# Routing spread over the projection in single steps, with VectorE and TensorE pinned to program order, in a decoder layer with a mixture of experts

## The chip, the core and the metric

The kernel runs on one core of one Trainium2 chip. A core has five engines with a queue each: TensorE (PE: matrix products and transposes), VectorE (DVE), ScalarE (ACT), GpSimd (POOL) and SyncE (SP, which only issues transfers here); POOL issues the gathers, which take their row numbers from a table. Each engine works off its queue in order and waits for the others by semaphores. The metric is the device time of one execution in microseconds (us), lower is better.

## The reference

A decoder layer on 16 sequences of 100 tokens of width 512 (1600 tokens): causal self-attention, cross-attention to 361 context rows for each sequence, and a feed-forward part with 8 experts, two for each token. A layer norm follows each part. The change touches the output product of the cross-attention, its layer norm, and the feed-forward part:

```python
# cross-attention, end
out = out.transpose(0, 2, 1, 3).reshape(b, s, NH * HD)   # 16 heads of 128
return out @ Wo                                          # 2048 x 512
...
# feed-forward, x is the normed sum
logits = jnp.einsum('bsd,de->bse', x, router_w) + router_b
topk_vals, topk_idx = jax.lax.top_k(logits, 2)
topk_w = jax.nn.softmax(topk_vals, axis=-1)
full_w = jnp.sum(one_hot(topk_idx, 8) * topk_w[..., None], axis=-2)
h = jnp.einsum('td,edf->etf', xf, expert_w) + expert_b[:, None, :]
combined = jnp.einsum('etf,te->tf', silu(h), full_w)
out = combined @ proj_w + proj_b
y = x + out
return norm_w * (y / sqrt(mean(y * y) + EPS))
```

With two choices, the softmax of the two greatest logits is a pair of gates g1 and g2 = 1 - g1.

## The kernel before

**Precision.** Most products are made of three: each operand is split into a high part (a cast, `split`, L135) and the rest (a subtraction, L142), and `mm3` (L145) sums high by high, high by low and low by high. The cast runs on ACT as a rule, the subtraction on DVE or POOL. So each operand of PE costs one operation on ACT and one on DVE or POOL.

**The output product.** The 1600 tokens are 13 tiles of 128 (the last has 64). A *part* (t, g) is tile t by head group g of four heads: `d_part` (L878) makes 4 x 3 products of 512 columns into the tile's sum `acc`. The list `parts` goes tile by tile for tiles 0 to 9 and then, for the last `TAIL` = 3 tiles, group by group: (10,0), (11,0), (12,0), (10,1) and so on; parts 40 to 51. `d_load(i+1)` (L869) is written ahead of `d_part(i)`: it fetches the heads (`of`) and splits them into `ot`, a pair with two buffers, with the subtraction on DVE for odd parts and on POOL for even ones. Behind the last group of a tile follows `d_norm` (L898): the residual is fetched and added, statistics on DVE, logarithm and exponential on ACT, the scaling on DVE, a store to `x2d`.

**Logits.** `d_turn(t)` (L980) transposes a normed tile on PE, copies it on ACT, adds the projection's bias on POOL and stores that to `xbd`. `d_logits` (L996) gives four small products, which are set among the products of a part, and one addition on DVE (`lg`).

**Routing** is exact and all on the chip. `choose(a, b)` (L1110) finds the two greatest logits for tiles a to b-1, and each token's rank in its expert: a chain of small DVE operations, then products with triangular matrices on PE into `gb`, then a second chain. `settle(a, b)` (L1204) assigns tiles of 128 places (slots) to experts, some 40 DVE operations on tables of 72 to 648 columns. `slots` (L1306) makes the row numbers `idx` and the offsets of each slot's expert (`wat`, `bat`) from 36 or more products of one or few columns. The first 9 tiles (`CUT`) are settled early and give the first 11 slots (`EARLY`) of 32; the other 21 slots need all 13 tiles.

**Experts.** The weights of expert e are split into slot e of an arena that holds `Wo`, too, so that four experts wait for the last part that reads their place (`load_expert`, L1389). For slot i, `e_gather` (L1348) fetches 128 rows by index on POOL's queue, `e_turn` (L1352) transposes them on PE and splits them on ACT and DVE, `e_product` (L1360) makes 12 products with weights at an offset read from `wat`, `e_bias` (L1373) fetches a bias on SP, `e_out` (L1378) adds it on DVE, applies silu on ACT and stores. After 32 slots each token's two rows are gathered, weighed by g1 and g2, projected and normed; that stage is not touched.

**Order.** The program is traced in the order of the code, and a scheduler then orders the instructions of each engine by priority (by place in the code, unless `tc.high_priority(offset=...)` lifts them) and by the times at which a model of the chip has them ready. `in_turn` (L122) adds an order between two instructions without a semaphore. In the code the routing is written as whole functions: `choose` behind tiles 3, 6 and 9, `settle` and `slots` behind part 39, `choose(CUT, CUT + 1)` behind part 42; the second round, for the last three tiles, behind expert product 2.

Of the kernel before, what the change touches and what calls it, by code (L numbers as in the profile page):

```python
# [63 lines left out]
def tile_decoder_layer(  # L64
# [69 lines left out]

    def split(dst, src, high=None, low=None):  # L135

        high, low = high or nc.scalar, low or nc.vector
        if high is nc.scalar:
            ins = nc.scalar.copy(dst.h, src)  # L139
        else:  # L140
            ins = high.tensor_copy(dst.h, src)  # L141
        low.tensor_tensor(dst.l, src, dst.h.bitcast(FP), ALU.subtract)  # L142
        return ins
# [836 lines left out]
    def d_turn(t):  # L980
        t0, n = TT[t]
        x2 = X2.pop(t)
        pt = bank("t", [128, KC, 128], f"ptx2_{t}")
        for k in range(KC):
            nc.tensor.transpose(
                pt[:, k, :n], x2[:n, k * 128 : (k + 1) * 128], ident[:n, :n]
            )
        if t < NT - 1:
            XT2[t] = w1.tile([128, KC, 128], FP, name=f"x2f_{t}", tag="x2f")
        else:  # L990
            XT2[t] = raw[:, 0].rearrange("p (k n) -> p k n", n=128)
        nc.scalar.copy(XT2[t][:, :, :n], pt[:, :, :n])
        nc.gpsimd.tensor_tensor(x2[:n], x2[:n], pb[:n], ALU.add)
        nc.sync.dma_start(xbd[t][:n], x2[:n])
# [114 lines left out]

    def choose(a, b):  # L1110
# [5 lines left out]
        for j in range(2):  # L1116

            nc.vector.tensor_reduce(top[:, j, a:b], vals, AX.X, ALU.max)
            hit = table("hit", sh)
            nc.vector.tensor_tensor(  # L1120
                hit, vals, top[:, j, a:b].unsqueeze(2).to_broadcast(sh), ALU.is_equal
            )
            nc.vector.tensor_tensor(hit, hit, num_b, ALU.mult)
            nc.vector.tensor_reduce(place[:, j, a:b], hit, AX.X, ALU.min)
            nc.vector.tensor_tensor(
                one[:, j, a:b, :],
                num_b,
                place[:, j, a:b].unsqueeze(2).to_broadcast(sh),
                ALU.is_equal,
            )  # L1130
            if j == 0:
                rest = table("rest", sh)
                nc.vector.scalar_tensor_tensor(
                    rest, one[:, 0, a:b, :], -BIG, vals, ALU.mult, ALU.add
                )
                vals = rest
        if b == NT:

            nc.vector.memset(one[64:, :, NT - 1, :], 0.0)
        nc.vector.tensor_tensor(  # L1140
            chosen[:, a:b, :], one[:, 0, a:b, :], one[:, 1, a:b, :], ALU.add
        )
        for t in range(a, b):
            nc.vector.tensor_tensor(
                cum[:, t + 1, :], cum[:, t, :], chosen[:, t, :], ALU.add
            )
        o1, o2 = 2 * NE, (2 + m) * NE
# [21 lines left out]
        )  # L1169
        sh2 = [128, 2, m, NE]  # L1170
# [6 lines left out]
        )  # L1177
        rj = gw.tile([128, 2, m], FP, name=f"rj_{a}", tag=f"rj_{m}")
        nc.vector.tensor_reduce(rj, mine, AX.X, ALU.add)
        ri = gw.tile([128, 2, m], I32, name=f"ri_{a}", tag=f"ri_{m}")  # L1180
        nc.vector.tensor_copy(ri, rj)
        nc.vector.tensor_scalar(ri, ri, 127, None, ALU.bitwise_and)
        nc.vector.tensor_copy(lo[:, :, a:b], ri)

        nc.vector.tensor_scalar(rj, place[:, :, a:b], float(NE), None, ALU.add)
        nc.vector.scalar_tensor_tensor(
            opens[:, :, a:b], lo[:, :, a:b], 0.0, rj, ALU.is_equal, ALU.mult
        )
        if b == NT:
            nc.vector.memset(opens[64:, :, NT - 1 :], 0.0)  # L1190
            nc.vector.memset(token[64:, NT - 1 :], 0.0)

        for j in range(2):
            for t in range(a, b):
# [7 lines left out]
                )  # L1202

    def settle(a, b):  # L1204
# [5 lines left out]
        if a == 0:  # L1210
            by_128(full, count[:, m, :], "full")

        up = table("up", [128, m + 1, NE])
        nc.vector.tensor_scalar(up, count, 127.0, None, ALU.add)
        had = table("had", [128, m + 1, NE])
        by_128(had, up, f"had_{a}")

        opn = table("opn", sh)
        nc.vector.tensor_tensor(opn, had[:, 1:, :], had[:, :m, :], ALU.subtract)
        had = had[:, :m, :]  # L1220
        sh4 = [128, m, NE, NE]

        def before_it(these, here, less, name):
# [7 lines left out]
            )  # L1231
            new = table(name, sh)
            nc.vector.tensor_reduce(new, part, AX.X, ALU.add)
            nc.vector.tensor_reduce(here[:, a:b], these, AX.X, ALU.add)
            tri = parts_of([128, 1, m, b])[:, 0]
# [5 lines left out]
            )  # L1241
            till = table("till", [128, m])
            nc.vector.tensor_reduce(till, tri, AX.X, ALU.add)
            nc.vector.scalar_tensor_tensor(
# [6 lines left out]
            )  # L1251
            return new


        new = before_it(opn, opened, 0 if a else -EARLY, "new")
        if a == 0:
# [3 lines left out]
            )  # L1260
            nc.vector.tensor_tensor(fills, fills, opn, ALU.mult)
            first = before_it(fills, filled, 0, "first")
# [3 lines left out]
            )  # L1266

            nc.vector.scalar_tensor_tensor(
                fills, first, float(EARLY), fills, ALU.is_lt, ALU.mult
            )  # L1270
            nc.vector.tensor_tensor(first, first, new, ALU.add)
            nc.vector.tensor_tensor(first, first, fills, ALU.mult)
            nc.vector.tensor_tensor(new, first, new, ALU.subtract)

        nc.vector.tensor_tensor(places[:, a:b, :], opn, new, ALU.mult)
        sh5 = [128, m, NE, b]
# [6 lines left out]
        )  # L1283
        old = table("old", sh)
        nc.vector.tensor_reduce(old, prior, AX.X, ALU.max)
        nc.vector.tensor_tensor(new, new, old, ALU.subtract)

# [3 lines left out]
        )  # L1291
        nc.vector.tensor_tensor(new, new, past, ALU.mult)
        nc.vector.tensor_tensor(new, new, old, ALU.add)
        sh3 = [128, m, NSL]
        for j in range(2):
            mine = table("chose", sh)
            nc.vector.tensor_tensor(mine, one[:, j, a:b, :], new, ALU.mult)
            nc.vector.tensor_reduce(tile_of[:, j, a:b], mine, AX.X, ALU.add)
            nc.vector.tensor_tensor(
# [4 lines left out]
            )  # L1304

    def slots(a, b, upto):  # L1306
# [4 lines left out]
        inv, who = gb[:, o1:o2], gb[0:1, o2:]  # L1311
        for dst, of in ((inv, named), (who, opens.unsqueeze(3))):
# [9 lines left out]
        nc.vector.tensor_copy(idx, inv)  # L1322
        wat = k1.tile([1, m], I32, name=f"wat_{a}")
        nc.vector.tensor_scalar(wat, who, float(KC * D), None, ALU.mult)
        bat = k1.tile([1, m], I32, name=f"bat_{a}")
        nc.vector.tensor_scalar(bat, who, float(D), None, ALU.mult)
        for i in range(a, b):
# [61 lines left out]
    def load_expert(e, last=False):  # L1389
        for k in range(KC):  # L1390
# [10 lines left out]
            )  # L1401

    for i in range(HEAD * NKV, len(parts)):
# [4 lines left out]
        if t < NT - TAIL:  # L1408
            if g == 1:
# [10 lines left out]
        elif (t, g) == (NT - 1, NKV - 1):  # L1420
            d_turn(NT - TAIL)
        d_part(i, among)
        if g == NKV - 1:
            with tc.high_priority(offset=URGENT if t >= NT - TAIL else 0):
                d_norm(t)
# [4 lines left out]
        if t % 3 == 0 and t <= CUT and g == 3:  # L1430
            choose(t - 3, t)
        if (t, g) == (NT - 1, 0):
            choose(CUT, CUT + 1)
        if (t, g) == (CUT, 3):
            settle(0, CUT)
            slots(0, EARLY, CUT)
        if (t, g) == (NT - 1, 1):
# [4 lines left out]
    load_expert(wo_slot[3], True)  # L1442
    e_turn(0)
    e_turn(1)
    e_product(0, d_logits(NT - TAIL))
    with tc.high_priority(offset=URGENT):
        d_turn(NT - 2)
        d_turn(NT - 1)
    e_turn(2)

    def at_once(t):
        with tc.high_priority(offset=URGENT):
            for f in d_logits(t).values():
                f()

    e_product(1, {1: lambda: at_once(NT - 1)})
    e_turn(3)
    e_product(2, {0: lambda: at_once(NT - 2)})
    d_l.close()
    e_l = ExitStack()  # L1460
    ebb = pool(e_l, "ebb")
    for i in range(TAIL):
        e_bias(i)
    for i in range(TAIL):
        e_out(i)
    with tc.high_priority(offset=URGENT):
        choose(CUT + 1, NT)
        settle(CUT, NT)
        slots(EARLY, NSL, NT)
    slot_f = gw.tile([128, 2 * NT], FP, name="slot_f")  # L1470
    nc.vector.scalar_tensor_tensor(
        slot_f,
        tile_of.rearrange("p j t -> p (j t)"),
        128.0,
        lo.rearrange("p j t -> p (j t)"),
        ALU.mult,
        ALU.add,
    )
    slot = k1.tile([128, 2, NT], I32, name="slot")
    nc.vector.tensor_copy(slot.rearrange("p j t -> p (j t)"), slot_f)  # L1480
    ex = gw.tile([128, NT], FP, name="ex")
    nc.vector.tensor_tensor(ex, top[:, 1, :], top[:, 0, :], ALU.subtract)
    nc.scalar.activation(ex, ex, AF.Exp)
    g1 = k1.tile([128, NT], FP, name="g1")
    nc.vector.tensor_scalar(g1, ex, 1.0, None, ALU.add)
    nc.vector.reciprocal(g1, g1)
    g2 = k1.tile([128, NT], FP, name="g2")
    nc.vector.tensor_tensor(g2, ex, g1, ALU.mult)
# [284 lines left out]
    for i in range(NSL + 1):  # L1773
        if i + 4 < NSL:
            e_gather(i + 4)
# [3 lines left out]
        if TAIL <= i < NSL:  # L1779
            e_product(i)  # L1780
            e_out(i)
        if i == EARLY + 1:
# [102 lines left out]
```

## Time and profile before

| what | us |
|---|---|
| three runs of the kernel | 1400.23, 1400.51, 1403.87 |
| the profiled execution | 1408.13 |
| its span, first to last instruction | 1406.4 |
| PE busy | 1331.6 |
| DVE busy | 942.8 |
| ACT busy | 756.4 |
| POOL busy | 710.3 |

The profile comes from one execution and has several views. The table of engines gives busy time for each engine; the table by stage gives the same for chosen stretches, with the clock that TensorE was granted (1.00 is full). The list of waits tells which instruction ended an engine's idle time. The timeline gives start, duration, engine, line, operation, output and inputs of each instruction, and in brackets the idle time ahead of it with what ended it; on PE the durations of neighbours overlap, and the pace is read from one start to the next. `acc` is the sum of a tile, `ot_h` and `ot_l` its split heads, `xs` and `xsT` gathered rows as they come and turned, `ph` an expert product, `parts`, `new`, `old` and `hit` tables of the routing.

In the profile the last product of tile 9 starts at 1161.0 us, the last part ends at 1205.2, and the product of slot 11 starts at 1260.9. Routing of the first 9 tiles ran on DVE from 1163 to 1201, that of the last three from 1225 to 1252.

### The profile page before, as it was taken

The numbers are of one execution on the slowest core, as the hardware profiler recorded it, in microseconds if no ns is written. First come the engines' busy times: TensorE is split into PE (matmuls) and PEld (weight loads), VectorE is DVE, ScalarE is ACT, GpSimd is POOL, SyncE is SP. The second block draws the span as 40 slices with busy tenths as digits, with TensorE's granted clock in tenths as the row PEclk, the third lists the DMA queues.
The fourth block names the chain that finished last, engine by engine and source line by source line (L and its number), as shares of the span: only waits on it lengthen the run. The fifth ranks groups of instructions, "written<-read, shape, count | busy, mean of one in ns | idle before, by whom it ended". The sixth has DMA issues, their size and how long they took to land.

```text
span 1406.4 us, 25135 instructions
## 1 busy us (share of the span) xinstructions
PE 1331.6 (95%) x7928; PEld 1105.0 (79%) x7928; DVE 942.8 (67%) x2933; ACT 756.4 (54%) x1897; POOL 710.3 (51%) x840
## 2 busy tenths in 40 slices
PE   8999989999999999999999999999999898899894
PEld 7888868888778888888888888878887676677773
DVE  5776677776467777777777767767654558754576
ACT  4666643444446666666666666656654233333356
POOL 6878753344245555555555555545455444532530
PEclk9999989999999999999999999999999999899997
DMA  5221363544442122322233312322446545667883
GB/s 170 68 74 58 124 194 96 131 92 114 100 94 72 42 70 71 76 78 70 71 76 78 74 46 67 73 68 51 118 101 182 178 167 164 211 214 240 256 252 118
DMA packets 199160, 161.74 MB, mean 115 GB/s; under 512 B 133581, under 2 KB 153265, under 8 KB 199029
## 3 DMA queue, kind: packets, MB, share of 16 engines
q1 hardware_dynamic: 189191, 139.77, 36.2%
q0 software_dynamic: 4576, 14.95, 3.4%
q10 hardware_dynamic: 5262, 5.41, 1.3%
q8 instruction: 65, 1.06, 0.3%
q14 instruction: 66, 0.54, 0.1%
HBM read 107.25 MB, written 50.99 MB: 113 GB/s over the span
## 4 chain that ended last, share of the span: by engine, by line
PE 68%; DVE 14%; DMA 7%; ACT 4%; issue 3%; POOL 1%; SPq 1%; ACTq 1%; DVEq 0%; POOLq 0%
PE pq L147 4%; PE pq L148 4%; PE pq L149 4%; PE pv L147 4%; PE pv L148 4%; PE pv L149 4%; PE ptp L819 3%; PE pk L147 3%; PE pk L149 3%; PE pk L148 3%; PE s L147 3%; PE s L148 3%; PE s L149 3%; PE av L148 2%; PE av L147 2%
## 5 line engine op out<-in xcount | busy, mean ns | idle before, releaser
L811 POOL TENSOR_SCALAR p<-p,sums 100x361 f32<-100x361 f32 x256 | 146.4, 577 | 99.4 <-DVE sums L810 88.2
L798 DVE CUSTOM_DVE_ANT_0 p<-s,nmask 100x361 f32<-100x361 f32 x256 | 133.0, 527 | 63.4 <-PE s L149 54.7
L809 ACT ACTIVATE p<-p,nm 100x361 f32<-100x361 f32 x256 | 153.2, 601 | 39.6 <-DVE nm L798 36.3
L142 DVE TENSOR_TENSOR pT_l<-ptp,pT_h 128x400 fp32r<-128x400 f32 (+1 forms) x192 | 107.5, 568 | 57.2 <-ACT pT_h L139 56.8
L147 PE MATMUL pq<-WH 128*128 128x512 f32 (+2 forms) x272 | 107.2, 394 | 5.3 <-DVE WH L141 5.3
L819 PE MATMUL ptp<-ident,p 100*128 100x100 f32 (+1 forms) x768 | 107.4, 252 | 0.0
L139 ACT CAST pT_h<-ptp 128x400 fp32r<-128x400 f32 (+1 forms) x192 | 91.2, 487 | 30.1 <-PE ptp L819 29.7
L142 POOL TENSOR_TENSOR cT_l<-cf,cT_h 128x512 fp32r<-128x512 f32 (+1 forms) x48 | 54.4, 1133 | 103.4 <-ACT cT_h L139 101.5
L819 PEld LDWEIGHTS ptp<-ident,p 100*128 100x128 f32 (+1 forms) x768 | 95.4, 151 | 13.3 <-POOL p L811 2.3
L148 PE MATMUL pq<-WL,WH 128*128 128x512 f32 (+2 forms) x272 | 104.9, 385 | 0.0
L149 PE MATMUL pq<-WH,WL 128*128 128x512 f32 (+2 forms) x272 | 104.6, 385 | 0.0
L149 PE MATMUL acc<-WH,ot_l 128*128 128x512 f32 (+1 forms) x208 | 85.7, 413 | 7.3 <-DVE ot_l L142 5.8
L147 PE MATMUL acc<-WH,ot_h 128*128 128x512 f32 (+1 forms) x208 | 85.1, 409 | 5.0 <-ACT ot_h L139 5.0
L147 PE MATMUL s<-kT_h,WH 128*100 128x362 f32 x256 | 88.1, 355 | 0.7 <-ACT kT_h L139 0.7
L147 PE MATMUL av<-pT_h,WH 128*128 128x400 f32 (+1 forms) x192 | 76.8, 400 | 9.0 <-ACT pT_h L139 8.6
L666 POOL TENSOR_TENSOR qs<-qs,r_q 128x512 f32<-128x512 f32 (+1 forms) x52 | 54.0, 1068 | 60.9 <-DVE r_q L171 49.4
L149 PE MATMUL s<-kT_h,WL 128*100 128x362 f32 x256 | 84.3, 329 | 0.0
L148 PE MATMUL s<-kT_l,WH 128*100 128x362 f32 x256 | 83.7, 327 | 0.0
L148 PE MATMUL acc<-WL,ot_h 128*128 128x512 f32 (+1 forms) x208 | 83.6, 402 | 0.0
L142 POOL TENSOR_TENSOR WL<-qf,WH 128x400 fp32r<-128x400 f32 x64 | 67.3, 1052 | 30.5 <-ACT WH L139 26.9
L147 PE MATMUL pv<-WH,cT_h 128*128 128x512 f32 (+1 forms) x192 | 79.8, 416 | 0.9 <-DVE WL L142 0.9
L148 PE MATMUL pv<-WL,cT_h 128*128 128x512 f32 (+1 forms) x192 | 77.9, 406 | 0.0
(348 smaller groups left out, 3990.6 us busy)
## 6 DMA issues: line engine op xcount, KB each, us to landing
qf<-qd SPq DMA_DIRECT2D x64, 200.0 KB
of<-od SPq DMA_DIRECT2D x48, 256.0 KB
cf<-in_ctxT SPq DMA_DIRECT2D x16, 722.0 KB
eb<-in_expert_b SPq DMA_DIRECT2D x32, 256.0 KB
ysd<-h SPq DMA_DIRECT2D x32, 256.0 KB
f_e<-in_expert_w SPq DMA_DIRECT2D x30, 256.0 KB
f_wq<-in_Wq SPq DMA_DIRECT2D x16, 256.0 KB
f_wo<-in_Wo SPq DMA_DIRECT2D x16, 256.0 KB
```

The costliest lines, as they stand in the source:

```text
L139: ins = nc.scalar.copy(dst.h, src)
L142: low.tensor_tensor(dst.l, src, dst.h.bitcast(FP), ALU.subtract)
L147: nc.tensor.matmul(out, a.h, b.h, start=start, stop=False)
L148: nc.tensor.matmul(out, a.h, b.l, start=False, stop=False)
L149: nc.tensor.matmul(out, a.l, b.h, start=False, stop=stop)
L666: nc.gpsimd.tensor_tensor(qr[:, hs, :], qr[:, hs, :], rs[:n, hs].unsqueeze(2).to_broadcast([n, GR, HD2]), ALU.mult,)
L798: nc.vector.tensor_tensor_reduce(out=p, in0=sc[:, :SE], in1=nmask, scale=1.0, scalar=BIG, op0=ALU.add, op1=ALU.min, accum_out=nm,)
L809: nc.scalar.activation(p, p, AF.Exp, bias=nm, scale=-1.0, accum_out=sh)
L811: nc.gpsimd.tensor_scalar(p, p, sh, 1.0, ALU.mult, ALU.mult)
L819: nc.tensor.transpose(pt[:n, h, :], probs[h][:, c0 : c0 + n], ident[:S, :S])
```

## The change

`choose`, `settle` and `slots` become generators that yield after each operation, and yield `PAUSE` ahead of their products on PE. `route(n)` takes n steps, over the list `routing`; a pause ends its turn, so that the products are traced behind the next part. It is called with 12 behind each part from part 12 to 48, with 15 and 14 around expert product 2, and with 11 behind each later product until the list is empty, which is behind product 7. `pin` then adds an order between each instruction and the one traced before it, on DVE and on PE, for all that was traced since part 12.

```diff
+    def route(n):
+        while n and routing:
+            what = next(routing[0], None)
+            if what is None and routing[0].gi_frame is None:
+                routing.pop(0)
+                continue
+            if what == PAUSE:
+                return
+            n -= 1
+
+    def pin(engine, since):
+        prev = None
+        for ins in nc.cur_bb.bb.instructions[since:]:
+            if ins.engine == engine:
+                if prev is not None:
+                    tc.add_manual_dep(
+                        ins,
+                        prev.name,
+                        mybir.DependencyInfo(
+                            mybir.DependencyClass.NoSync, mybir.DependencyReason.DATA
+                        ),
+                        reason="pin",
+                    )
+                prev = ins
...
             nc.vector.tensor_reduce(top[:, j, a:b], vals, AX.X, ALU.max)
+            yield
...
             nc.vector.tensor_tensor(
                 cum[:, t + 1, :], cum[:, t, :], chosen[:, t, :], ALU.add
             )
+            yield
+        yield PAUSE
```

The loop over the parts (the turn of the tile before moves from group 1 to group 2; the rows of slots 0 and 1 are turned ahead of parts 50 and 51; the norm of tile 12 moves behind the loop; the lifted priorities go):

```diff
-            if g == 1:
+            if g == 2:
                 d_turn(t - 1)
...
         elif (t, g) == (NT - 1, NKV - 1):
             d_turn(NT - TAIL)
+            e_turn(1)
+        elif (t, g) == (NT - 2, NKV - 1):
+            e_turn(0)
         d_part(i, among)
-        if g == NKV - 1:
-            with tc.high_priority(offset=URGENT if t >= NT - TAIL else 0):
-                d_norm(t)
+        if g == NKV - 1 and t < NT - 1:
+            d_norm(t)
...
         if t % 3 == 0 and t <= CUT and g == 3:
-            choose(t - 3, t)
+            routing.append(choose(t - 3, t))
+        if (t, g) == (CUT, 3):
+            routing += [settle(0, CUT), slots(0, EARLY, CUT)]
         if (t, g) == (NT - 1, 0):
-            choose(CUT, CUT + 1)
-        if (t, g) == (CUT, 3):
-            settle(0, CUT)
-            slots(0, EARLY, CUT)
-        if (t, g) == (NT - 1, 1):
+            routing.append(choose(CUT, CUT + 1))
+        if i == PINNED:
+            since = traced()
+        if i < len(parts) - TAIL:
+            route(12)
+        if i == len(parts) - TAIL - 1:
+            assert not routing
             for k in range(4):
                 e_gather(k)
```

Behind the loop the order is written anew. POOL's addition and the store of `xbd` become a function `d_bias`, which for the last three tiles is called later and is held behind the subtraction of the last expert's first row of weights:

```diff
+    at_once(NT - TAIL)
+    d_turn(NT - 2)
     load_expert(wo_slot[3], True)
-    e_turn(0)
-    e_turn(1)
-    e_product(0, d_logits(NT - TAIL))
-    with tc.high_priority(offset=URGENT):
-        d_turn(NT - 2)
-        d_turn(NT - 1)
+    at_once(NT - 2)
+    d_norm(NT - 1)
+    e_product(0)
     e_turn(2)
+    e_gather(4)
+    d_turn(NT - 1)
+    d_bias(NT - TAIL)
+    d_bias(NT - 2)
+    for i in range(TAIL):
+        e_bias(i)
+    e_out(0)
     e_product(1, {1: lambda: at_once(NT - 1)})
     e_turn(3)
-    e_product(2, {0: lambda: at_once(NT - 2)})
+    e_gather(5)
+    d_bias(NT - 1)
+    e_out(1)
     d_l.close()
...
-    with tc.high_priority(offset=URGENT):
-        choose(CUT + 1, NT)
-        settle(CUT, NT)
-        slots(EARLY, NSL, NT)
+    routing += [choose(CUT + 1, NT), settle(CUT, NT), slots(EARLY, NSL, NT)]
+    route(15)
+    e_product(2)
+    e_out(2)
+    route(14)
...
             e_product(i)
             e_out(i)
+            if routing:
+                route(11)
+                if not routing:
+                    slot, g1, g2 = gates()
+                    for e in (nc.vector.engine, nc.tensor.engine):
+                        pin(e, since)
+            while len(SLOT) > asked[0] < min(i + 5, NSL):
+                e_gather(asked[0])
+                asked[0] += 1
```

The gates take a hyperbolic tangent in place of an exponential and a reciprocal:

```diff
-    nc.vector.tensor_tensor(ex, top[:, 1, :], top[:, 0, :], ALU.subtract)
-    nc.scalar.activation(ex, ex, AF.Exp)
-    g1 = k1.tile([128, NT], FP, name="g1")
-    nc.vector.tensor_scalar(g1, ex, 1.0, None, ALU.add)
-    nc.vector.reciprocal(g1, g1)
-    g2 = k1.tile([128, NT], FP, name="g2")
-    nc.vector.tensor_tensor(g2, ex, g1, ALU.mult)
+        nc.vector.tensor_tensor(th, top[:, 0, :], top[:, 1, :], ALU.subtract)
+        nc.scalar.activation(th, th, AF.Tanh, scale=0.5)
+        g1 = k1.tile([128, NT], FP, name="g1")
+        nc.vector.tensor_scalar(g1, th, 0.5, 0.5, ALU.mult, ALU.add)
+        g2 = k1.tile([128, NT], FP, name="g2")
+        nc.vector.tensor_scalar(g2, th, -0.5, 0.5, ALU.mult, ALU.add)
```

## The prediction

> **What bounds the kernel now.** I read the table of engines first, then its slices, then a table by stage of the part that the change touches, then PE's waits there, then the instructions in order of time. The table of engines:
>
> ```profile
> PE 1331.6 (95%) x7928; PEld 1105.0 (79%) x7928; DVE 942.8 (67%) x2933; ACT 756.4 (54%) x1897; POOL 710.3 (51%) x840
> ```
>
> PE is busy 95% of the span, so a change can win only where PE idles, and where its clock falls after idling. The table by stage says where (columns: stretch, its length, busy time and instructions of PE, PE's weight loads, DVE, ACT, POOL; granted clock; DMA share, GB/s):
>
> ```profile
> 1090.00:1161.00 71.00, 64.14 (x302) 50.63 (x301) 37.62 (x113) 21.09 (x43) 31.42 (x24) 0.98 0.52 171
> 1161.00:1205.00 44.00, 38.77 (x195) 27.69 (x194) 38.02 (x98) 14.73 (x30) 25.65 (x21) 0.92 0.53 160
> 1205.00:1261.00 56.00, 50.28 (x289) 40.24 (x287) 37.03 (x127) 21.23 (x37) 23.13 (x25) 0.89 0.71 227
> ```
>
> The first stretch is the product of the output for tiles 3 to 9 (parts 12 to 39), the second its last twelve parts (40 to 51), the third the last turns and logits, the second routing and expert products 0 to 10. In the second DVE is busy 38.0 of 44 us, nearly as long as PE: there DVE is the bound. PE's idle time, by the waits: 6.9 us in the first (3.65 us of it for ACT, below, and 0.65 just behind it), 5.3 in the second, some 6 in the third. In order of time, three of them:
>
> ```profile
> 1108.01 0.50 PE L147 MATMUL acc<-WH,ot_h 128*128 128x512 f32 x1 [3.65 <-ACT ot_h L139]
> ...
> 1145.30 0.63 PE L985 MATMUL ptx<-ident,x 128*128 128x128 f32 x4 [1.10 <-DVE x L183]
> ...
> 1182.45 0.69 PE L149 MATMUL acc<-WH,ot_l 128*64 128x512 f32 x1 [3.60 <-DVE ot_l L142]
> ```
>
> The last is the stall that the change can act on: an `ot_l` stood in DVE's queue behind a burst of routing.
>
> **The change on DVE and PE, first the ends of tiles.** Pinned program order means that the DVE half of a split runs only after all that was written before it. The split for part (t+1, 1) is written at the head of iteration (t+1, 0), hence behind `d_norm(t)`, which can't start before the last product of tile t, and behind the routing steps of that iteration. In the trace of before it is let through in the middle of the norm (DVE, tile 9; routing lines left out):
>
> ```profile
> 1161.45 0.69 DVE L904 TENSOR_TENSOR x<-acc,x 128x512 f32<-128x512 f32 x1 [4.97 <-PE acc L149]
> 1162.06 0.68 DVE L142 TENSOR_TENSOR ot_l<-of,ot_h 128x512 fp32r<-128x512 f32 x1
> 1162.65 0.16 DVE L1008 TENSOR_TENSOR lg<-gb,rb 128x8 f32<-128x8 f32 x1
> 1162.73 0.69 DVE L177 BATCH_NORM_STATS2 st_ln<-x 128x6 f32<-128x512 f32 x1
> ...
> 1164.99 0.54 DVE L183 TENSOR_SCALAR x<-x,mv_ln,r_ln 128x512 f32<-128x512 f32 x1
> ```
>
> Worked out for the changed order: PE's stream leaves tile 9 at 1161.4 (its last product starts at 1161.0 and a logits product follows). A part is 12 products at 0.233 us from start to start (1130.16, 1130.39, 1130.62 in the trace), 2.8 us; so part (t+1, 0) lasts until 1164.2, and the third product of part (t+1, 1) needs its `ot_l` at 1161.4 + 2.8 + 0.5 = 1164.7. DVE: `lg` 0.15, then `x<-acc` from 1161.7 to 1162.4, then statistics to the end of `x` 2.8 us as above (1162.73 to 1165.53), so 1165.2, then `ot_l` 0.7: 1165.85. **Stall 1.15 us at each tile's end**, six of them for tiles 3 to 8: 6.9 us. Behind tiles 3 and 6 twelve steps of `choose` come first. They take 0.214 us each one behind the other (five spacings from 1128.08 to 1129.15), 2.6 us: +5.2 us. The turn moved from the second to the third part of a tile no longer waits for the norm; that removes the 1.10 above and a 0.30 at 1115.07.
>
> After the pause `choose` sends its matmuls behind a whole part on PE, and twelve more steps lie ahead of the next `ot_l`. PE has 3.6 us of work there (a turn 0.35, a part 2.8, two products 0.5). The steps took 5.15 us in the trace (1134.21 on: `mine` 0.70, `ri` 0.67 and 1.21, four `named` 1.7, the rest under 0.2) and come to 2.5 if none is held up; with 0.25 for the handover and 0.7 for `ot_l` the stall is 0 to 2.5 us. I take the middle, 1.2, twice: 2.4 us.
>
> **The clock** is granted by PE's own activity. The rule of the Trainium skill (TensorE: Matmul & The Clock Gate, "What's actually happening") is that half clock comes after an idle window of about 3.4 us, and that the windows run freely. By that a gap of 3.75 us seldom fills a window and would cost nothing more. The trace is harsher: behind the 3.65 us at 1104 the next 4 us were granted 0.57, behind the 1.10 us at 1144 the clock stayed 1.00. I go by the row: 1.15 costs itself, and the two stalls of 1.15 + 2.6 = 3.75 us another 1.7 each (half of 3.4), 3.4 in all. By the rule it would be 0.
>
> Stage one: 6.9 + 5.2 + 2.4 + 3.4 = 17.9 us, in place of 6.9 idle and 1.7 of half clock = 8.6. The ACT stall at 1104 (casts of expert weights ahead of `ot_h`, waiting for their DMA) is not undone by the change, but it lies 2.6 to 6.3 us behind the end of tile 3, within the new stall there, so I don't count it twice. **+9 us** (+7 to +12).
>
> **The last twelve parts.** Between two `ot_l` on DVE PE does two parts, 5.6 us. The change puts 24 routing steps there; beside 0.7 for the split each may take 0.2. But `settle` has big ones:
>
> ```profile
> 1189.53 1.46 DVE L1278 TENSOR_TENSOR parts<-places,earlier 128x648 f16<-128x648 f32 x1
> 1191.02 0.83 DVE L1285 TENSOR_REDUCE old<-parts 128x72 f32<-128x648 f16 x1
> 1191.89 0.98 DVE L1286 TENSOR_TENSOR new<-new,old 128x72 f32<-128x72 f32 x1
> 1192.90 0.23 DVE L1292 TENSOR_TENSOR new<-new,past 128x72 f32<-128x72 f32 x1
> ```
>
> DVE ran without a break from 1171.2 to 1198.7, 27.5 us; less 5.6 for the rest of `choose` and 2.7 for three splits, `settle` took 19.2 us. Here a second rule (SBUF — State Buffer, "Who interferes with whom": VectorE and GpSimd lock one pair of ports, the second to come is blocked for the whole instruction) tells why one `i_full` of 8 columns took 1.29 and its neighbour of 80 columns 0.19: POOL's subtractions take 1.28. By the rule any of some 40 steps can lose 1.3 us; by the rows without hold-up they sum to 13.5, as run 19.2. I keep both ends.
>
> From the end of tile 9: norm 4.0, twelve steps 2.6, `ot_l` 0.7, so PE gets on at 7.3 and reaches `choose`'s matmuls at 9.9; then 3.1 to 5.6 for its second half, 0.9 for `lg` and a split, 13.5 to 19.2 for `settle`, 0.7 for a split: the slots' matmuls at 28.1 to 36.3, some 1 later with handovers. PE, held by each split, is only at the end of part 46 then. Behind that: slots 1.2, five parts 14.0, `choose(CUT)`'s matmuls 0.3, two turns of gathered rows 0.7, the turn of tile 10 0.35 with a wait of 0.9 for its norm: 17.5. Sum 46.7 to 55.1, and 1.7 to 3.4 for the clock, 48.4 to 58.5 against 44.0 now: +4 to +15, **middle +9**. The gathers issue at about 31 to 39 and are needed three parts later; a gather took 1.19 to issue and was used 5.3 us after its start, so they are just in time.
>
> **The tail, where the change wins.** Now 55.7 us pass from the last part (1205.2) to product 11 (1260.9). In the changed order turns 0 and 1 and `choose(CUT)` are already paid. Product 0 still needs the last expert's split: ready 4.9 us behind the last part now (1210.1), kept at 5.0, since `lg` now stands ahead of it on DVE. Eleven products of 2.8: 30.8; eleven turns of 0.35: 3.9; turn and logits of tile 12, and the matmuls of routing, 3.0; wait for tile 12's norm 0.9. Sum 43.6; one period of half clock 2.5 (there are two now) and DVE steps late for a split 1.5: 47.6. The slots are known behind product 7 in place of product 8, so the gather that PE waits for now (0.65 us, after 1.10 for the one before) is nearly covered. **−8 us** (−5 to −11).
>
> **Moves at nothing.** The gates: DVE 3 operations for 4, one activation either way; the table loads around `ex` (1.28 us each, at 1224.6 and 1231.0) may go, but no PE wait ends on them. If that cover were gone, 2.6. The stores of `xbd` and POOL's additions for tiles 10 to 12 go behind the weights: POOL is freed for 3.9 us, and these stores are read in the last stage only. On SP the biases and `x1d` of tile 12 move with their steps; the biases wait for slots known since part 46. The gathers of slots 4 and 5 stay on POOL's queue behind their turns. Beyond product 11 nothing changes, and the 0.2 to 3 us waits there stay.
>
> **Sum:** +9 + 9 − 8 = **+10 us**. The profiled execution was 1408.1 (span 1406.4, 1.7 around it), which makes it 1418; the median of the runs shown is 1400.5, so I say 1410.5.
>
> **The rivals.** (1) *The burst was the damage, and steps heal it*: if a step costs 0.2 us, all 24 fit between two splits. Place: parts 40 to 51. Then PE loses there only the first 2.4 and 0.9 us: some 38 us, −6; stage one without clock loss and hold-ups 12.1 in place of 8.6, +3.5; the tail −10: 1388. For it: the 3.60 us stall ended on just such a burst, and small steps do run at 0.21. Against: 41 steps as run average 0.47. It decides if the steps of `settle` average under 0.2 us. (2) *Stalls change places*: the low ends, +7 + 4 − 11 = 0: 1400. (3) *Gathers late as well*: POOL's weight splits (four at 1.3 us) ahead of the first gather would make part 50 wait some 3 us behind turn 0, and the clock 2 more; with the high ends in the parts, +12 + 12 + 5 − 7 = +22: 1422. That the pins bind nothing has no sign in the code.
>
> **Chances.** Forecast (+5 to +17) 0.49; (3) 0.15; (2) 0.12; (1) 0.24. What a measurement can tell from no change is 0.3%, 4.2 us. Faster 0.24, same 0.12, slower 0.64. The range takes in half of (1): 1387 to 1426; the forecast's own is 1405 to 1418.
>
> **What would show it.** Right: waits of `acc` for DVE's `ot_l` at each end of a tile, over 1 us, 3 to 4 where `choose` follows; part 51 ending 4 to 15 us later than now relative to tile 9; product 11 closer to part 51 by 8. Wrong: PE's waits for `ot_l` gone between 1161 and 1205, or DVE taking the split ahead of the norm.

## The result, and the profile after

The changed kernel takes **1455.4 us** (median of 4 runs, 1451.28 to 1458.22) against 1400.4 for the kernel before (4 runs beside it, 1397.98 to 1403.87): ratio **1.0384, interval 1.0355 to 1.0414**, so 3.8% slower. The profiled execution took 1458.22 us, its span 1456.4, 50.0 us more than the span of 1406.4 before. The side was forecast rightly, the size was not: 10 us were forecast, and the time lies above the whole range.

The table of engines and two rows of the slices of the changed kernel:

```profile
PE 1345.6 (92%) x7928; PEld 1112.6 (76%) x7928; DVE 953.8 (65%) x2932; ACT 755.5 (52%) x1895; POOL 713.2 (49%) x840
...
PE   8999989999999999999999999999967686889995
...
PEclk9999989999999999999999999999979898899997
```

Every engine has the work it had. PE is busy 14.0 us longer with the same 7928 matmuls, which is a lower clock, and idles 36 us more. The dent of 6 to 8 tenths lies in five slices of 36.4 us, 1056 to 1238 us: the first part of the stretch that was pinned.

To divide the 50 us I cut both traces at the same events: 1060 us (attention ending; 164 products of `acc` had started by then in the old trace, 168 in the new), the end of tile 9, the last part, the start of product 11. The table by stage of the kernel before (columns as in the prediction: stretch, length, PE, PE's weight loads, DVE, ACT, POOL, clock, DMA):

```profile
1060.00:1161.50 101.50, 93.36 (x457) 74.92 (x455) 51.48 (x155) 33.48 (x70) 46.38 (x43) 0.98 0.57 181
...
1205.30:1260.90 55.60, 49.89 (x287) 39.91 (x286) 36.71 (x126) 20.89 (x37) 22.85 (x24) 0.89 0.71 227
1260.90:1406.00 145.10, 118.53 (x536) 92.93 (x536) 85.40 (x256) 69.21 (x143) 39.54 (x42) 0.91 0.68 216
```

and of the changed kernel, all four stages:

```profile
1060.00:1200.80 140.80, 103.11 (x445) 81.78 (x444) 58.75 (x153) 32.36 (x68) 46.22 (x43) 0.85 0.41 128
1200.80:1261.50 60.70, 46.20 (x209) 31.71 (x209) 47.29 (x129) 16.88 (x34) 28.97 (x24) 0.83 0.46 144
1261.50:1315.30 53.80, 45.91 (x265) 35.09 (x263) 31.05 (x94) 15.90 (x29) 20.12 (x21) 0.94 0.64 206
1315.30:1456.00 140.70, 117.41 (x536) 92.48 (x536) 86.13 (x256) 70.53 (x144) 41.30 (x42) 0.91 0.70 223
```

| stage | before | after | difference | forecast |
|---|---|---|---|---|
| 1060 us to the end of tile 9 | 101.5 | 140.8 | **+39.3** | +9 |
| the last twelve parts | 43.8 | 60.7 | **+16.9** | +9 |
| last part to product 11 | 55.6 | 53.8 | **-1.8** | -8 |
| product 11 to the end | 145.1 | 140.7 | -4.4 | 0 |

The first stage alone outweighs everything else. Length less PE's busy time gives PE's idle time there: 8.1 us before, 37.7 after, **+29.6**. PE's busy time for nearly the same matmuls (457 and 445 recorded) grows from 93.4 to 103.1, **+9.7**, at a clock of 0.85 in place of 0.98. PE's waits, in order of time:

```profile
1075.56 1.08 PE L987 MATMUL ptx<-ident,x 128*128 128x128 f32 x4 [11.59 <-DVE x L185]
...
1096.97 0.56 PE L151 MATMUL acc<-WH,ot_l 128*128 128x512 f32 x1 [4.24 <-DVE ot_l L144]
...
1114.18 0.69 PE L151 MATMUL acc<-WH,ot_l 128*128 128x512 f32 x1 [2.02 <-DVE ot_l L144]
...
1135.74 0.80 PE L151 MATMUL acc<-WH,ot_l 128*128 128x512 f32 x1 [5.98 <-DVE ot_l L144]
...
1155.46 0.79 PE L151 MATMUL acc<-WH,ot_l 128*128 128x512 f32 x1 [4.25 <-DVE ot_l L144]
...
1176.28 0.79 PE L151 MATMUL acc<-WH,ot_l 128*128 128x512 f32 x1 [5.68 <-DVE ot_l L144]
...
1191.31 0.50 PE L151 MATMUL acc<-WH,ot_l 128*128 128x512 f32 x1 [0.95 <-DVE ot_l L144]
```

The six `ot_l` are the forecast stalls behind tiles 3 to 8, 23.1 us in sum; two more of 0.51 lie between them and make 24.1 us of waits for DVE's `ot_l`. A wait of 1.00 for ACT's `ot_h` comes on top. The first line is a wait that the forecast does not have at all: the turn of a normed tile, 11.59 us, with 0.73 behind it for the turned tile's copy. Together 37.5, nearly all of the 37.7 us of idle time.

**The 11.59 us.** The timeline of all engines around it shows where the norm of tiles 1 and 2 hangs (SPq is SP's issue of a transfer; "x2", "x3" are neighbours drawn together):

```profile
1062.66 1.39 SPq L905 DMA_DIRECT2D x<-x1d  x3
...
1068.19 1.29 DVE L906 TENSOR_TENSOR x<-acc,x 128x512 f32<-128x512 f32 x2 [4.91 <-DMA x<-x1d]
...
1074.87 1.15 DVE L185 TENSOR_SCALAR x<-x,mv_ln,r_ln 128x512 f32<-128x512 f32 x2
```

Three residuals `x1d` are issued together at 1062.66, when attention ends; DVE waits 4.91 us for them, and the normed tiles are there at 1076. PE does products of `acc` as filler beside attention, and in the kernel before it went on with them: 53 start between 1060 and 1077. In the changed trace none does. PE stopped after exactly 168, which is parts 0 to 13: the turn of tile 2 is written ahead of part 14, and a pinned PE may not pass it.

**The 6 us behind tiles 5 and 7.** The same view, around the stall at 1135.74:

```profile
1131.31 0.62 ACT L141 CAST WH<-f_e 128x512 fp32r<-128x512 f32 x1 [2.33 <-DMA f_e<-in_expert_w]
1131.84 0.20 ACT L161 ACTIVATE a_ln<-v_ln 128x1 f32<-128x1 f32 x1
...
1132.68 0.61 DVE L165 SCALAR_TENSOR_TENSOR t_ln<-y_ln,v_ln 128x1 f32<-128x1 f32 x1 [5.60 <-ACT y_ln L162]
```

The norm's logarithm (`a_ln`) stands on ACT behind casts of expert weights that wait for their transfer. DVE waits 5.60 us for it inside the norm, and the `ot_l` behind it in DVE's list waits too. In the kernel before DVE took `ot_l` in the middle of such a norm.

### The profile page after: what moved, and what is told of

The parts are those of the page before. It is cut to its first block, busy times and chain, and to the rows that moved or that the text cites. A ratio compares the mean times of both kernels' runs of the same rounds, so it can differ in the third digit from the quotient of the medians.

```text
span 1456.4 us, 25126 instructions
## 1 busy us (share of the span) xinstructions
PE 1345.6 (92%) x7928; PEld 1112.6 (76%) x7928; DVE 953.8 (65%) x2932; ACT 755.5 (52%) x1895; POOL 713.2 (49%) x840
## 3 DMA queue, kind: packets, MB, share of 16 engines
q8 instruction: 65, 1.06, 0.3%
## 4 chain that ended last, share of the span: by engine, by line
PE 69%; DVE 15%; DMA 8%; ACT 4%; issue 3%; POOL 1%; SPq 1%; ACTq 0%; DVEq 0%; POOLq 0%
PE pq L149 4%; PE pq L150 4%; PE pq L151 4%; PE pv L149 4%; PE pv L150 3%; PE pv L151 3%; PE ptp L821 3%; PE pk L149 3%; PE pk L151 3%; PE pk L150 3%; PE s L149 3%; PE s L150 3%; PE s L151 2%; PE acc L151 2%; PE acc L149 2%
## 5 line engine op out<-in xcount | busy, mean ns | idle before, releaser
L800 DVE CUSTOM_DVE_ANT_0 p<-s,nmask 100x361 f32<-100x361 f32 x256 | 133.2, 528 | 63.2 <-PE s L151 54.5
L811 ACT ACTIVATE p<-p,nm 100x361 f32<-100x361 f32 x256 | 153.2, 601 | 38.7 <-DVE nm L800 35.4
L151 PE MATMUL acc<-WH,ot_l 128*128 128x512 f32 (+1 forms) x208 | 91.4, 439 | 34.1 <-DVE ot_l L144 33.2
L149 PE MATMUL acc<-WH,ot_h 128*128 128x512 f32 (+1 forms) x208 | 93.3, 449 | 1.0 <-ACT ot_h L141 1.0
L150 PE MATMUL acc<-WL,ot_h 128*128 128x512 f32 (+1 forms) x208 | 88.5, 425 | 0.0
L141 ACT CAST ot_h<-of 128x512 fp32r<-128x512 f32 (+1 forms) x52 | 31.3, 601 | 102.2 <-PE acc L150 67.4
L144 POOL TENSOR_TENSOR WL<-qf,WH 128x400 fp32r<-128x400 f32 x64 | 67.8, 1060 | 30.4 <-ACT WH L141 26.8
L151 PEld LDWEIGHTS acc<-WH,ot_l 128*128 128x128 f32 (+1 forms) x208 | 42.3, 204 | 50.4 <-DVE ot_l L144 37.8
```

Of the source, the lines that this page charges most:

```text
L144: lows[0] = low.tensor_tensor(dst.l, src, dst.h.bitcast(FP), ALU.subtract)
L149: nc.tensor.matmul(out, a.h, b.h, start=start, stop=False)
L150: nc.tensor.matmul(out, a.h, b.l, start=False, stop=False)
L151: nc.tensor.matmul(out, a.l, b.h, start=False, stop=stop)
L800: nc.vector.tensor_tensor_reduce(out=p, in0=sc[:, :SE], in1=nmask, scale=1.0, scalar=BIG, op0=ALU.add, op1=ALU.min, accum_out=nm,)
L811: nc.scalar.activation(p, p, AF.Exp, bias=nm, scale=-1.0, accum_out=sh)
```

## The experiments

The kernel before measured 1405.0, 1409.2 and 1405.2 us beside the runs below, so only ratios to it are compared. Markers in us (the end of tile 9, and so on) are from one profiled execution each. Every edit is to the changed kernel, but for the last.

### Which pin, and over what

**No pin.** Steps, written order, gates and all the rest stay; only `pin` is not called.

```diff
-                    for e in (nc.vector.engine, nc.tensor.engine):
+                    for e in ():
```

> The changed kernel without any pin: steps, moved turns, tanh and the rewritten order behind the parts stay, the scheduler orders all. Theory: near the kernel before, 1394 to 1408 us. Rival (steps are the cost): over 1440 us.

Measured: **1.0038, 1.0022 to 1.0053**. Tile 9 ends at 1161.65 (before: 1161.45), the last part 48.8 us later. The steps and the new order cost 0.4%; the pins cost the other 3.4%.

**Pins from part 39 on**, so that parts 12 to 38 are left to the scheduler.

```diff
-    PINNED = 3 * NKV
+    PINNED = 10 * NKV - 1
```

> The changed kernel, both pins, but only from part 39 on in place of part 12. Theory (the pins cost some 39 us ahead of the end of tile 9, and some 12 in the last twelve parts against the kernel without pins): the end of tile 9 comes at 1160 to 1164 in place of 1201, the last twelve parts still take 58 to 63 us: 1414 to 1424 us. Rival (only the start of the pinned stretch costs, and any start costs as much): over 1430 us.

Measured: **1.0040, 1.0027 to 1.0054**, the same as with no pin. Against the changed kernel that is 1.0384 / 1.0040 = 1.034: the pins over parts 12 to 39 cost about 48 us, those behind them nothing in sum. The last twelve parts took 56.2 us here, less than expected, and the tail to product 11 54.5; with no pin they took 48.8 and 57.4.

**DVE alone**, `for e in (nc.vector.engine,)`, **and PE alone**, `for e in (nc.tensor.engine,)`, both from part 12.

> The changed kernel with the pin on VectorE only. Theory (its loss has two sources: TensorE, pinned, can no longer run ahead of the turn of tile 2, 11.6 us idle and some 4 of half clock; VectorE, pinned, holds the splits behind norms and routing): the 11.6 us wait goes, the waits of acc for ot_l at the tiles' ends stay at 2 to 6 us: 1436 to 1444 us. Rival (routing in single steps of normal priority is itself the cost, whatever the pins): unchanged, 1450 to 1458 us.

> The changed kernel with the pin on TensorE only. Theory: the wait of about 11.6 us for the turn of tile 2 stays, the waits for ot_l at the tiles' ends fall under 1 us, parts 40 to 51 come near 44 us: 1410 to 1422 us. Rival (steps are the cost): 1450 to 1458 us.

Measured: DVE alone **1.0359, 1.0320 to 1.0398**; PE alone **1.0193, 1.0155 to 1.0230**. Over no pin that is 3.2% and 1.5%, and both together 3.4%: the two overlap. Either expectation was too low, since I had given each pin its own waits. With PE alone the first wait stays (11.42 us); with DVE alone it falls to 4.28, but DVE's list now makes PE wait at turns (3.77, 2.47, 5.21 and 4.77) where PE's list made it wait at `ot_l`. So DVE's order is the larger cost and nearly enough by itself.

### The wait at 1075 us

**Pins from part 20 on**, when the residuals are long there.

```diff
-    PINNED = 3 * NKV
+    PINNED = 5 * NKV
```

> The changed kernel, both pins, from part 20 on in place of part 12. Theory (pinned at part 12, TensorE can't go on with parts 14 to 19 while the residual of tile 2 is fetched behind the end of attention): the 11.6 us wait and its half clock go, and the waits behind tiles 3 and 4: 1424 to 1436 us. Rival (the wait moves to the next turn): a wait of 8 us or more near 1075 stays, over 1445 us.

Measured: **1.0246, 1.0195 to 1.0296**; 1.3% less than the changed kernel, the low end of what was expected (the kernel before took 1409.2 us beside this run). The 11.6 us are gone and the last product of tile 3 ends at 1070.6 us (kernel before: 1069.9, changed kernel: 1089.2), but 5.43 us at 1099 (`ptx`, DVE's list standing at `place`) and 5.32 at 1112 (`gb` for `x2f`) appear, and tile 9 ends only 11.6 us earlier than in the changed kernel. A part of the wait moved to where the pins begin.

### The stalls at the ends of tiles

**The subtraction on POOL** for parts 13 to 39, so that no `ot_l` of them stands in DVE's list.

```diff
-        split(..., low=nc.vector if i % 2 else nc.gpsimd)
+        split(..., low=nc.vector if i % 2 and not 12 < i < 40 else nc.gpsimd)
```

> The changed kernel with every subtraction ot_l of parts 13 to 39 on POOL, so that none stands in DVE's pinned list. Theory (of the 48 us that the pins over parts 12 to 39 cost, the waits for DVE's ot_l with the clock behind them are about half, the run-ahead at 1064 us the rest): no wait of acc for DVE between 1076 and tile 9, the wait of 11.6 us stays, ratio 1.012 to 1.024. Rival (POOL's list is as late, since its subtraction takes 1.3 us and blocks DVE, or PE then waits for the turn and for chosen in DVE's list): ratio above 1.030.

Measured: **1.0212, 1.0185 to 1.0239**, 1.7% less than the changed kernel. This run's table by stage to the end of tile 9, and then the sums of PE's waits there:

```profile
1060.00:1174.80 114.80, 95.97 (x455) 77.62 (x454) 46.57 (x142) 33.82 (x69) 62.36 (x56) 0.93 0.52 160
```

```profile
PE ptx L987 <- DVE x L185: 9.7, 1, 9.7
PE gb L1208 <- DVE chosen L1196: 4.2, 2, 2.1
PE acc L151 <- POOL ot_l L144: 2.1, 4, 0.8
```

The stage is 26.0 us shorter (114.8 against 140.8), and of the 18.8 us that PE still idles half is the first wait: 9.7 us, once. The 24.1 us of waits for DVE's `ot_l` have become 2.1 us for POOL and 4.2 for `chosen`; with no stall of 4 to 6 us at a tile's end the clock is 0.93, not 0.85. So `ot_l` in DVE's list was the cause of these stalls, and clock was lost with them. DVE also has less to do here (46.6 us busy for 58.8); the next run keeps the work on DVE and changes only its place.

**The split written ahead of the norm** (part (t, 1) loaded ahead of `d_norm(t - 1)`, tiles 4 to 9):

```diff
+    EARLIER = [(t, 0) for t in range(4, NT - TAIL)]
...
-        if i + 1 < len(parts):
+        if i + 1 < len(parts) and (t, g) not in EARLIER:
             d_load(i + 1)
...
+        if (t, g) == (t, NKV - 1) and parts[i + 1 : i + 2] and parts[i + 1] in EARLIER:
+            d_load(i + 2)
```

> The changed kernel, both pins; only the split of part (t, 1) is written ahead of the norm of tile t-1, for tiles 4 to 9. Theory (the waits at the tiles' ends are the split's place behind the norm and routing in VectorE's queue): the waits of acc for VectorE's ot_l right behind tiles 3 to 8 (4.2, 2.0, 6.0, 4.3, 5.7, 1.0 us) fall under 1 us each, the 11.6 us wait stays: 1424 to 1438 us. Rival (the waits come from VectorE's total load or from a clock that falls anyway): 1446 us or more, with waits in the same places or handed to the turns.

Measured: **1.0238, 1.0206 to 1.0269**. The waits for `ot_l` fall from 24.1 us to one of 5.54, and tile 9 ends 17.8 us earlier. Not all goes: PE now waits for `chosen` (2.54 and 3.49) and for turns (1.85 and 0.77). The first wait, which this edit was not to touch, fell from 11.59 to 7.34 us, so a few of the 17.8 us are not the split's; the runs don't say why it fell.

**Both repairs** (part 20, and the split ahead of the norm):

> The changed kernel with two repairs at once: pins from part 20 on in place of part 12, and each first-but-one split of a tile written ahead of the norm before it. Each alone brought 1.4 to 1.5%. Theory (the costs of the pins are separate waits with separate causes, so the gains add): ratio to the kernel before 1.007 to 1.014. Rival (in a pinned list PE waits for whatever stands next, so that one wait removed uncovers the next, and the gains don't add): ratio 1.018 to 1.025, with waits of gb or ptx in place of those for ot_l.

Measured: **1.0153, 1.0126 to 1.0179**, between the two expectations. In the first stage the gains do add (11.6 and 17.8 us singly): tile 9 ends at 1165.4, 35.4 us earlier than in the changed kernel and 4 later than in the one before. Two waits for the routing's list stay (5.77 for `hit`, 3.58 for `chosen`). But the last twelve parts take 63.5 us against 56.2 with pins from part 39; of what this version loses to that one (1.0153 against 1.0040, some 16 us), 7.3 lie there and 7.2 in the first stage.

**Weights later**: the expert weights of tiles 6 and 8 loaded two groups later, so that their casts don't stand ahead of the norms of tiles 5 and 7.

```diff
-            if g == 0 and t in (2, 4, 6, 8):
+            if g == (0 if t < 6 else 2) and t in (2, 4, 6, 8):
```

> The changed kernel, both pins; the expert weights loaded in tiles 6 and 8 are loaded at their third part, not at their first. Theory (behind tiles 5 and 7 the norm's logarithm and exponential stand in ScalarE's queue behind casts of weights that wait for their transfer, and that makes 6.0 and 5.7 us of 1 to 2): these two waits fall to 1 to 2.5 us: 1441 to 1450 us. Rival (the casts don't matter): waits of 5 us or more stay behind tiles 5 and 7, 1451 to 1458 us.

Measured: **1.0368, 1.0343 to 1.0393**, no gain that can be told. The stalls behind tiles 5 and 7 fall to 1.99 and 2.02 as expected, but those behind 6 and 8 rise to 8.20 and 5.78. The casts explain the 6 us, and shifting them only shifts the stall.

### The tail alone

**Both pinned from the last part on** (`PINNED = len(parts) - 1`), **and PE alone from there**.

> The changed kernel with both pins, but only from behind the last part (51) to expert product 7. Theory: the stretch up to the last part is as without pins, and the tail keeps what the changed kernel gained behind the last part (2 to 6 us): 1392 to 1404 us, not slower than without pins by more than 4. Rival (the pins of the tail cost, too): slower than without pins by 5 to 10 us.

> The changed kernel with PE alone pinned, from the last part on; DVE is left to the scheduler. Theory (the written order of PE in the tail is good, since with PE alone pinned from part 12 the tail took 49.3 us against 55.7 before, and what makes the tail long when both are pinned from there, 64.4 us, is DVE's order): last part at 1210, tail 49 to 55 us, 140 us behind product 11, span 1399 to 1405, ratio 0.995 to 1.000. Rival (a pinned PE waits at the last part for a turn whose norm DVE does late, 7.07 us with both pinned): ratio 1.005 to 1.012.

Measured: both **1.0088, 1.0060 to 1.0116**; PE alone **1.0033, 1.0016 to 1.0050**. Both expected gains failed: the first is slower than no pin by 0.5%, some 7 us, as its rival said. From the last part to product 11 it is 64.7 and 59.5 us, not 49 to 55. A norm again, with both pinned:

```profile
1214.12 1.22 DVE L165 SCALAR_TENSOR_TENSOR t_ln<-y_ln,v_ln 128x1 f32<-128x1 f32 x1
1215.27 0.68 DVE L144 TENSOR_TENSOR WL<-f_e,WH 128x512 fp32r<-128x512 f32 x1
1215.87 1.74 DVE L144 TENSOR_TENSOR WL<-raw,WH 128x512 fp32r<-128x512 f32 x1
...
1218.38 0.55 DVE L185 TENSOR_SCALAR x<-x,mv_ln,r_ln 128x512 f32<-128x512 f32 x1
1218.98 0.71 PEld L987 LDWEIGHTS ptx<-ident,x 128*128 128x128 f32 x4 [7.16 <-DVE x L185]
```

DVE splits the last expert's weights between two steps of the norm of tile 11, some 3 us of the 7 that PE's turn waits (7.07; the line shows its weight load). Ahead of them the norm's exponential stood 1.8 us on ACT behind a cast that waited for its transfer. The short tail of 49.5 us that PE alone had when pinned from part 12 came at the price of 61.9 us for the last twelve parts, in which those norms were done: 111.4 in sum, against 99.4 before. So the written order in the tail is no gain by itself, and no version here is faster than the kernel before.

### The small edits

**The kernel before with the turn at group 2 and the gates by tanh**, nothing else of the change.

> The kernel before with two parts of the change alone: the turn of the tile before at group 2 in place of group 1, and the gates by tanh. Theory (both cost nothing, as the prediction has it): within 0.3% of the kernel before, ratio 0.997 to 1.003; the waits of ptx for DVE's x (1.10 and 0.30 us) gone. Rival (they are why the changed kernel is 4 us shorter behind product 11, and two table loads less and 1.4 us of turns count): ratio 0.994 to 0.997.

Measured: **0.9996, 0.9977 to 1.0014**. Both cost nothing, as the prediction had it; the wait of a turn for its norm did not vanish, though (0.96 us at 1143 for 1.10). This profiled execution took 139.7 us behind product 11 and the kernel before 145.1, at equal medians: single executions differ there by more than the 4.4 us of the table, so these stay unexplained.

## Why the prediction was right and wrong

**What bounds the kernel, and the side.** Right: DVE's order under a pin makes PE wait where the scheduler had let work pass, and the tail does not pay for it.

**Stage one, +9 forecast, +39.3 measured: the step that failed.** The sum held only stalls of 1.15 to 3.75 us at tile ends. It put the loss of run-ahead at the start of the pinned stretch at nothing, and it took every norm as 4.0 us long.

- *The start of the pinned stretch.* I put parts 12 to 39 at 1090 to 1161 us and costed only the ends of tiles there. But pins hold from part 12 in the written order, and PE was past part 12 at 1060 us already. What the scheduler did between 1060 and 1077, running ahead into products while the norms waited for their residuals, was not in the sum: 12.3 us of idle time (11.59 + 0.73), and a clock of 0.50 until 1083.6. The row that I read could show no sign of it, since it began at 1090, when 253 products, 21 parts, had started.
- *The stalls at the ends of tiles, 14.5 us forecast (6.9 + 5.2 + 2.4), 24.1 measured.* The mechanism is right in each, and the size is near where no cast is in the way: 4.24 and 4.25 behind tiles 3 and 6 against 1.15 + 2.6 = 3.75. Two errors partly cancel in it: the norm took 3.5 us, not 4.0, and one of the twelve steps, `hit`, took 1.04 beside POOL's split where its like take 0.18. Behind tiles 5 and 7 ACT's casts of weights stretch the norm to 9.8 and 7.2 us, and the stalls are 5.98 and 5.68 for 1.15. The trace of before had signs of this. The wait of 3.65 us for such casts at 1104 lies behind tile 5 (300 products, 25 parts, had started), not behind tile 3, where the prediction put it and so left it out; and the norms of tiles 5 and 7 took 12.7 and 10.1 us from first step to last. The expected stall behind the second half of `choose` came to no more than 0.51, for 1.2.
- *The clock, 3.4 us forecast.* The 1.7 us for each of the two stalls of 3.75 came out: behind tiles 3 and 6 PE worked 3.40 and 3.24 us at 0.50, and half of that is lost. What the sum lacked is the clock behind the other gaps:

```profile
1075.50:1083.60 8.10, 8.04 (x28) 7.00 (x29) 2.21 (x5) 0.70 (x2) 5.54 (x7) 0.50 0.55 189
1097.30:1100.70 3.40, 3.40 (x9) 2.67 (x8) 0.08 (x1) 0.00 (x0) 0.00 (x0) 0.50 0.45 150
1131.40:1141.60 10.20, 5.86 (x16) 4.73 (x17) 3.59 (x6) 2.19 (x6) 2.77 (x3) 0.50 0.30 77
1155.30:1158.70 3.40, 3.24 (x8) 2.57 (x9) 0.50 (x4) 0.00 (x0) 0.00 (x0) 0.50 0.45 154
1175.80:1179.20 3.40, 2.92 (x7) 2.35 (x8) 0.42 (x1) 0.00 (x0) 0.00 (x0) 0.50 0.43 143
```

With the 3.40 us behind tile 4 (last section) the other four gaps had 20.2 us of work at 0.50 behind them, 10.1 us lost.

**Where the 48 us of the pins are.** They don't divide into independent shares. In the runs, taking `ot_l` out of DVE's list is worth 1.7%, starting at part 20 1.3%, a split ahead of the norm 1.4%; but DVE's pin alone costs nearly what both cost.

**The last twelve parts, +9 forecast, +16.9 measured.** With parts 12 to 38 free it is 56.2 us, +12.4, inside the forecast 48.4 to 58.5. The bursts stayed bursts under the pin, as the forecast (and not rival 1) had it. DVE, between two `ot_l` at 1215 and 1230 in the changed kernel:

```profile
1219.21 1.20 DVE L1110 CAST full<-i_full 128x8 f32<-128x8 int32 x1
...
1221.95 0.20 DVE L1110 CAST had<-i_had 128x80 f32<-128x80 int32 x1
...
1222.46 0.76 DVE L1300 TENSOR_TENSOR parts<-lower,opn 128x576 f16<-128x576 f32 x1
...
1225.41 1.80 DVE L1300 TENSOR_TENSOR parts<-lower,fills 128x576 f16<-128x576 f32 x1
```

The same kind of step takes 1.20 and 0.20, or 1.80 and 0.76, the long ones while POOL subtracts (1219.10 and 1225.34, 1.27 and 1.26 us). 14.3 us pass between the two splits, PE waits 6.81 for the second, and the slots' products come 38.4 us behind tile 9, where 28.1 to 36.3 and some 1 for handovers were forecast. The 4.5 us over the 56.2 go with the pinned stage ahead; the runs don't say how.

**The tail, -8 forecast, -1.8 measured.** PE's busy time fell by 4.0 us (49.9 to 45.9), but its idle time rose from 5.7 to 7.9. I allowed 1.5 us for splits late behind routing steps; the waits for `rank` and `xsT_l` are 1.24, 1.55 and 1.16. A turned tile's copy, product 0 and a gathered row's cast add 0.68, 0.77 and 0.84 where I had 0.9 in all.

**Rivals.** None gave the size. Rival 1 is refuted: steps alone, without pins, end the last part 48.8 us behind tile 9 (before: 43.8), not earlier. Rival 2, the low ends (+7, +4, -11), lies below what each stage measured. Rival 3 is not what happened: no wait for gathered rows over 0.4 us in the tail.

## What to carry to other kernels

A pinned order forbids every overtaking, also that which no one planned: before pinning, list what the scheduler runs ahead of its written place, at the start of the stretch above all, and what each head of a queue would then wait for (another engine's casts and their transfers included). Price a pin by the slowest chain ahead of each operand, not by one clean instance: in the trace of before the norms took from 3.6 to 12.7 us. An operand that PE needs soon does better on an engine whose list holds no long chain: here POOL, at 1.3 us for DVE's 0.7, gave back 26.0 of the 39.3 us that the stage had lost.

## What the runs showed of the hardware

**A gap of 2 us can be enough for half clock, by its place.** The rows of the changed kernel around the stall of 2.02 us that ends at 1114.18:

```profile
1112.00:1114.30 2.30, 0.28 (x2) 0.12 (x2) 2.12 (x2) 0.17 (x1) 1.33 (x1) 1.00 0.30 114
1114.30:1117.70 3.40, 3.40 (x9) 2.64 (x10) 0.00 (x0) 0.00 (x0) 0.00 (x0) 0.50 0.49 154
1117.70:1121.00 3.30, 3.30 (x18) 2.72 (x17) 1.56 (x1) 1.11 (x2) 1.30 (x1) 0.99 0.02 6
```

PE has 9 products in 3.40 us at 0.50, then 18 in 3.30 at 0.99: the gap of 2.02 costs 1.7 us more. The Trainium skill (TensorE: Matmul & The Clock Gate, "What's actually happening") asks for an idle window of about 3.4 us, by which this gap would be free; the measurement decides. In and behind the long wait of 11.59 it was 0.50 for 17.1 us (1066.5 to 1083.6), so 8.0 us of work behind the wait ran at half speed.

Not every such gap costs. The run with the weights later has two of the same length, each with the row behind it:

```profile
1131.30 0.50 PE L151 MATMUL acc<-WH,ot_l 128*128 128x512 f32 x1 [1.99 <-DVE ot_l L144]
1132.30:1135.70 3.40, 3.40 (x12) 2.67 (x10) 0.06 (x1) 0.62 (x1) 0.00 (x0) 0.50 0.52 152
...
1171.63 0.50 PE L151 MATMUL acc<-WH,ot_l 128*128 128x512 f32 x1 [2.02 <-DVE ot_l L144]
1173.30:1176.70 3.40, 3.40 (x18) 2.77 (x18) 0.64 (x1) 1.11 (x2) 1.29 (x1) 1.00 0.42 118
```

What differs is the place. In each trace the half-clock stretches begin and end on a grid of 3.41 us: in the changed kernel at 1066.5, 1083.6, 1097.3, 1100.7, 1114.3, 1117.7 and on, all a whole number of such steps apart. By this run's own grid the gap of 1.99 us lies inside one step (1128.9 to 1132.3), while that of 2.02 is cut by an edge at 1169.9, which leaves 1.76 us of idle time in the step behind it. So a grid of free-running windows agrees with the page; that a window must be idle throughout does not. What a gap of about 2 us costs is in part chance, and a forecast can only give both ends. A gap of 1.10 us alone in its step left the clock at 1.00 (kernel before, ending at 1145.30).

**The shared ports reach the split itself.** In the stall behind tile 4, from the timeline of the changed kernel:

```profile
1112.24 1.33 POOL L144 TENSOR_TENSOR ot_l<-of,ot_h 128x512 fp32r<-128x512 f32 x1 [5.74 <-ACT ot_h L141]
1112.37 1.75 DVE L144 TENSOR_TENSOR ot_l<-of,ot_h 128x512 fp32r<-128x512 f32 x1
```

DVE's subtraction, 0.69 us alone, takes 1.75 beside POOL's, since the stall lets both parts' splits come due at once; it ends 0.55 us behind POOL's. This row agrees with the lock that the prediction cites, and its 1.06 us are more than the difference between the stall forecast there, 1.15, and the one measured, 2.02. The section cited there excepts reductions on this chip, so "any of some 40 steps" was too wide; in the run with no pin a reduction (`old`, 128x416) takes 0.58 us while POOL works, and in the run pinned from part 39 0.59 while POOL idles.
